# The RWKV recurrence's two exponentials from one clipped difference, and nine small operations of the routing scheduled later

## The chip, the cores and the metric

The kernel runs as one program on one core of a Trainium2 chip. The time is the device time of one execution in microseconds, from its start to the end of its last instruction or transfer. The kernel before was timed nine times: median 370.09 us, lowest 368.94, highest 377.28. The profile beside these times is that of one more execution.

A core has five engines that run at the same time, each through its own list of instructions in order: TensorE (PE: matrix products, with weight loads listed as PEld), VectorE (DVE), ScalarE (ACT), GpSimd (POOL) and SyncE (SP, which here only issues transfers). They wait for each other by semaphores.

## The reference

One layer on 2048 tokens of 512 channels. The normalised input goes into two parts, whose results are added to the input.

```python
xn = _layernorm(x)
# part 1: time mixing; a sequence of 2048 steps in every channel
r, v, k = split(einsum('btc,dc->btd', xn, W_rvk))
def step((p, q, o), (kt, vt)):              # w = -exp(time_decay), u = time_first
    no = maximum(o, u + kt)
    A, Bc = exp(o - no), exp(u + kt - no)
    y = (A * p + Bc * vt) / (A * q + Bc)
    no2 = maximum(w + o, kt)
    A2, B2 = exp(w + o - no2), exp(kt - no2)
    return (A2 * p + B2 * vt, A2 * q + B2, no2), y
attn = einsum('btc,dc->btd', sigmoid(r) * y, W_out)
# part 2: 12 experts, the two likeliest for each token; 8 are real (gate, up, down), 4 return their input
g, u = einsum(xn, gate_w), einsum(xn, up_w)
ffn = sum over the two experts of weight * (down_w of (silu(g) * u)), or weight * xn
out = x + attn + ffn
```

What the change touches is `no2`, `A2` and `B2`: one of the two exponents is always zero, since `no2` is the larger of `w + o` and `kt`.

## The kernel before

**Blocks and units.** The tokens are in four blocks of 512 (b = 0 to 3), the channels in four groups of 128 (c = 0 to 3). The recurrence is worked on in 16 units (b, c), in the order of b, then c: channels on the 128 partitions, 512 steps along the row. `scan(b, c)` is a unit. VectorE copies the state of the group into column 0 of the tile `obv` (L355); a hardware scan gives the maxima `o2` (L359); two operations make the exponents `a2` = w + o - o2 (L361) and `b2` = k - o2 (L362); ScalarE takes the two exponentials in place (L364, L365). Then the scan for the denominators (L371), the product with v (L372), the scan for the numerators (L373), the copies of the last column into the state (L380, L381), three operations that make the quotient's parts (L383 to L385), and the reciprocal in two halves with a product behind the second (L389, L391), which gives `yT`. In all but the last three units the halves are put off and done where `divide_some` is called.

**Products.** Keys, values and receptances of block 0 are made by plain products and by `seven`, those of blocks 1 to 3 by `pair`: seven products instead of eight for a product of 2 x 2 blocks (a scheme like Strassen's), for three matrices side by side. Its order on TensorE is written out in `pair`:

```python
order = "A1 A5 R1 A6 A2 R5 A7 A3 R6 A4 B1 R2 B5 B6 R7 B3 B7 R3 B2 B4 R4".split()
```

Every such product is a pair of passes at L601 (128 x 256), into one of the PSUM banks of `change_banks`: tags gu, p2, p3 and pr have one buffer, p1 has two, and `ps_o` (expert results and the output product) two. Products 2 are added to their destination by VectorE two steps later (`owe`, L633 for one of them); only then is bank p2 free for the next product 2. Most others are copied out by ScalarE (L612 to L645).

**Experts.** 23 tiles of 128 tokens are gathered by GpSimd (L1043, four indirect transfers to a tile, five tiles ahead), turned by VectorE (`turn`, L1101), multiplied by gate and up weights (`up`, L1120, 32 passes of 128 x 128 to a tile), put through the activation (`activate`: ScalarE L1132, VectorE L1133 and L1134), multiplied by the down weights (`finish`, L1085, two passes of 128 x 512), scaled by ScalarE (L1152) and added into the output by GpSimd (L1156). SP fetches the expert's weights, whose number it reads from a table on the chip. Two tiles, the fourth and the eighth, are mixed: their last 32 rows belong to another expert. `mixed_tiles` makes what they need, nine small VectorE operations (L999 to L1019): `late_i`, the addresses of those rows, and `owner_i`, the numbers of the experts, which SP reads in `fetch`.

**Order.** From the normalisation on, the order on every engine is the order in which the program emits instructions (a manual schedule), and in the main stage this comes from a table of due times: `plan(at, work)` lists a generator under a time; the table is sorted, and each entry advances its generator by one step, that is to its next `yield`. The 16 `scan` generators have six steps each: one spacing for the first unit, (-1, 3, 5, 7, 10, 11.5), and for the others (0, 5, 7.5, 9.5, 12, 14) after the unit's start, units being 16.75 apart. `mixed_tiles` is one step, due at 8, in the midst of the first unit; the expert tiles' halves, the products' steps and the output product of blocks 0 to 2 (`attention`, L1253) stand in the same table. The due times are only an order; nothing waits for a clock.

**End.** After the last units of block 3 only the output product of block 3 is left: sixteen groups of four passes at L1253 (the last group in two halves at L1241), each needing `yT` of all four channel groups of its block. Ahead of them on TensorE stand the output products of the rest of block 2.

Of the kernel before, what the change touches and what calls it, by code (L numbers as in the profile page):

```python
# [26 lines left out]
F32 = mybir.dt.float32  # L27
BF16 = mybir.dt.bfloat16
I32 = mybir.dt.int32
AF = mybir.ActivationFunctionType  # L30
ALU = mybir.AluOpType
# [3 lines left out]
P = 128  # L35
# [3 lines left out]
TB = 512  # L39
# [24 lines left out]
def layer(ctx: ExitStack, tc: tile.TileContext, x, w_rvk, w_out, decay, first, cls, ebias, gu, down, out):  # L64
    nc = tc.nc

    def pool(name, bufs, **kw):
        return ctx.enter_context(tc.tile_pool(name=name, bufs=bufs, **kw))
# [141 lines left out]
    for c in range(CC):  # L210

        s = const.tile([P, 5], F32, tag=f"state{c}", name=f"state{c}")
# [131 lines left out]
    def scan(b, c):  # L344

        n = f"{b}_{c}"
        s = state[c]
        w, cf = wdec[:, c : c + 1], cfac[:, c : c + 1]
        k = kvr[b, c, "k"]
        if c == 0:  # L350
            yT[b] = xyp.tile([P, CC, TB], F32, tag="xy", name=f"yT{b}")


        obv = wk1.tile([P, 3, TB + 1], F32, tag="obv", name=f"obv{n}")
        nc.vector.tensor_copy(obv[:, :, 0:1], s[:, 0:3].unsqueeze(2))  # L355
        o, bs, bvs = (obv[:, m, 0:TB] for m in range(3))
        o2, b2, bv = (obv[:, m, 1 : TB + 1] for m in range(3))

        nc.vector.tensor_tensor_scan(o2, w.to_broadcast([P, TB]), k, s[:, 0:1], ALU.add, ALU.max)  # L359
        a2 = wk1.tile([P, TB], F32, tag="a2", name=f"a2{n}")  # L360
        nc.vector.scalar_tensor_tensor(a2, o, w, o2, ALU.add, ALU.subtract)  # L361
        nc.vector.tensor_sub(b2, k, o2)  # L362
        yield
        nc.scalar.activation(a2, a2, AF.Exp)  # L364
        nc.scalar.activation(b2, b2, AF.Exp)  # L365
        yield

        v = kvr[b, c, "v"]
        sums = wk1.tile([P, 2, TB], F32, tag="sums", name=f"sums{n}")
        sq, sp = sums[:, 0, :], sums[:, 1, :]  # L370
        nc.vector.tensor_tensor_scan(sq, bs, a2, s[:, 3:4], ALU.add, ALU.mult)  # L371
        nc.vector.tensor_mul(bv, b2, v)  # L372
        nc.vector.tensor_tensor_scan(sp, bvs, a2, s[:, 4:5], ALU.add, ALU.mult)  # L373

        er = kvr[b, c, "r"]
        if b > 0:
            nc.scalar.activation(er, er, AF.Exp, scale=-1.0)
        num = yT[b][:, c, :]
        if b + 1 < NTB:
            nc.vector.tensor_copy(s[:, 0:3].unsqueeze(2), obv[:, :, TB : TB + 1])  # L380
            nc.vector.tensor_copy(s[:, 3:5].unsqueeze(2), sums[:, :, TB - 1 : TB])  # L381
        yield
        nc.vector.scalar_tensor_tensor(sq, b2, cf, sq, ALU.mult, ALU.add)  # L383
        nc.vector.scalar_tensor_tensor(er, er, 1.0, sq, ALU.add, ALU.mult)
        nc.vector.scalar_tensor_tensor(num, bv, cf, sp, ALU.mult, ALU.add)  # L385
        yield
        def divide(h):
            hs = slice(h * HALF, (h + 1) * HALF)
            nc.vector.reciprocal(er[:, hs], er[:, hs])  # L389
            if h == 1:  # L390
                nc.vector.tensor_mul(num, num, er)  # L391

        for h in range(2):
            divisions.append(lambda h=h: divide(h))
            if (b, c) in units[-3:]:
                divide_some(len(divisions))
                yield
# [4 lines left out]
    def divide_some(n):  # L402
        for _ in range(min(n, len(divisions))):
            divisions.pop(0)()
# [514 lines left out]
    for m, tok in enumerate((tok0, tok1)):  # L919
# [20 lines left out]
        for j in range(NT):  # L940
            k = m * NT + j
# [332 lines left out]
    wk1 = pool("wk1", 1)  # L1274
# [19 lines left out]
    head = False  # L1294
    fill(8)
    stages = [scan(*u) for u in units]
    DONE = 7 + 9 + 16 + 2 + 12
    STEPS = 2 * 2 * CC + 11 * (CC - LEAD) + 21 * (len(units) - CC) // 2
# [8 lines left out]
    def plan(at, what, *args):  # L1307
        table.append((at, iter([(what, *args)]) if callable(what) else what))

    for at in (-1, 3, 5, 7, 10, 11.5):  # L1310
        plan(at, stages[0])
    for u in range(1, len(units)):
        for at in (0, 5, 7.5, 9.5, 12, 14):
            plan((u - 1) * UNIT + 10.5 + at, stages[u])

    middle = attention(NTB - 2)
# [2 lines left out]
            plan((len(units) - 2) * UNIT + 10.5 + at, middle)  # L1319
    plan(3, gather, 3)  # L1320
    plan(3.5, turn, 0)
    plan(8, mixed_tiles)
    plan(4.5, gather, 4)
    one = total / groups / CC
    for m in range(groups):
# [35 lines left out]
    with tc.If(count > TILES):  # L1361
        with tc.For_i(TILES, MAX_TILES, 1) as i:
            cols = {}
            for name, a, dt in (
                ("which", which_i, I32), ("token", token_i, I32), ("to", to_i, I32), ("weight", wplace, F32)
            ):
                if name == "token":
                    shape, at = [P, P // SQ, 1], a[:, :, bass.ds(i, 1)]
                else:
                    shape, at = [P, 1], a[:, bass.ds(i, 1)]  # L1370
# [59 lines left out]
```

## Time and profile before

| what | value |
|---|---|
| median of nine executions | 370.09 us |
| all nine | 377.28, 368.94, 370.74, 369.48, 376.86, 370.63, 369.77, 370.09, 369.48 |
| the profiled execution | 370.26 us, of which the span of the profile is 368.4 |
| PE busy | 358.0 us, 97% of the span |
| VectorE busy | 320.0 us, 87% |
| GpSimd busy | 167.6 us, 45% |
| ScalarE busy | 116.9 us, 32% |
| granted TensorE clock, mean over the span | 0.991 |

By stages, as busy microseconds of each stretch:

| stretch, us | PE | VectorE | ScalarE | GpSimd | clock | DMA share |
|---|---|---|---|---|---|---|
| 0 to 20 (load, normalise) | 18.43 | 14.70 | 9.14 | 7.06 | 1.00 | 0.92 |
| 20 to 60 (first products, routing) | 39.64 | 34.72 | 18.30 | 2.90 | 1.00 | 0.72 |
| 60 to 110 (first units, first expert tiles) | 44.94 | 39.24 | 13.22 | 29.97 | 0.93 | 0.52 |
| 110 to 340 (main stage) | 230.00 | 212.55 | 74.52 | 120.60 | 1.00 | 0.73 |
| 340 to 368 (last units, last output product) | 24.95 | 18.81 | 1.75 | 7.05 | 1.00 | 0.76 |

A row of a group of instructions in the profile reads: line, engine, operation, output and inputs by their names in the program, shapes, count, then busy us and mean ns of one, and the idle time of the engine ahead of them with what ended it. A row of the timeline reads: start in us, length, engine, line, operation, and in brackets how long the engine had waited and for whom. Busy time of PE is modelled from the passes' starts, so a PE at 10.00 of 10 can still pass slowly: the distance between passes shows it.

### The profile page before, as it was taken

Reading aid. Unit: us, or ns where it says so; the run is one execution under the profiler, and the core shown is the slowest. Engines: PE = TensorE matmul, PEld = TensorE weight load, DVE = VectorE, ACT = ScalarE, POOL = GpSimd, SP = SyncE. Lnnn points to the kernel's source line nnn. Section 1 sums busy time; section 2 is a strip of 40 time slices with the busy share of each in tenths; the row PEclk is TensorE's granted clock in tenths of the full one; section 3 lists DMA queues with packets and bytes.
Section 4 is the critical chain, followed back from the end, with each engine's and each line's share of the span. In section 5 each row is a group of like instructions: output and inputs, shape, how many; then the busy total and the mean of one; then the engine's idle time right before and its main releaser. Section 6 shows DMA issues by size and latency. Waiting matters only on the chain. (4 is left out here: it accounts for less than half of the span.)

```text
span 368.4 us, 5356 instructions
## 1 busy us (share of the span) xinstructions
PE 358.0 (97%) x1854; PEld 259.7 (70%) x1854; DVE 320.0 (87%) x555; ACT 116.9 (32%) x263; POOL 167.6 (45%) x192
## 2 busy tenths in 40 slices
PE   8999999999789999999999999999999999999996
PEld 3765577898467679656777788888877788874444
DVE  5879889989389999699999798999999599989981
ACT  3576231333033333323341324432432334231100
POOL 7000300587655756556545186346788522113510
PEclk9999999999969999999999999999999999999999
DMA  7998940439454699666987676697879765933793
GB/s 262 397 390 332 342 142 0 145 86 405 167 190 98 178 337 294 230 165 196 306 286 221 201 213 191 185 246 219 263 229 236 198 163 149 315 55 36 176 187 115
DMA packets 25004, 78.69 MB, mean 214 GB/s; under 512 B 4368, under 2 KB 4752, under 8 KB 21200
## 3 DMA queue, kind: packets, MB, share of 16 engines
q1 hardware_dynamic: 16560, 58.28, 44.9%
q0 software_dynamic: 8416, 20.06, 26.2%
q8 instruction: 15, 0.25, 0.3%
q14 instruction: 13, 0.11, 0.1%
HBM read 63.25 MB, written 19.27 MB: 224 GB/s over the span
## 5 line engine op out<-in xcount | busy, mean ns | idle before, releaser
L1043 POOL DMA_INDIRECT xg<-xs,token_i x92 | 102.8, 1118 | 71.9 <-DVE token_i L984 27.7
L1120 PEld LDWEIGHTS pg<-xgT,gw 128*128 128x128 f32 x672 | 79.6, 194 | 3.4 <-issue 2.2
L1120 PE MATMUL pg<-xgT,gw 128*128 128x128 f32 x672 | 79.8, 277 | 0.0
L1156 POOL DMA_INDIRECT out_dram<-yo,to_i x23 | 39.8, 1732 | 66.4 <-issue 36.6
L1253 PE MATMUL pw<-wout_sb,yT 128*128 128x512 f32 x120 | 54.2, 595 | 0.2 <-PEq L1361 0.2
L389 DVE RECIPROCAL r<-r 128x256 f32<-128x256 f32 x32 | 53.7, 1718 | 0.0
L1085 PE MATMUL po<-dw,act 128*128 128x512 f32 x84 | 40.2, 595 | 0.9 <-issue 0.7
L1253 PEld LDWEIGHTS pw<-wout_sb,yT 128*128 128x128 f32 x120 | 22.2, 190 | 25.7 <-issue 24.5
L1132 ACT ACTIVATE act<-pg 128x256 f32<-128x256 f32 x23 | 8.8, 383 | 80.3 <-PE pg L1120 52.8
L601 PE MATMUL p<-S,wrvk 128*128 128x256 f32 x96 | 25.0, 379 | 1.9 <-issue 1.8
L1152 ACT ACTIVATE yo<-po,wplace 128x512 f32<-128x512 f32 x23 | 15.8, 688 | 34.2 <-PE po L1085 27.2
L1133 DVE SCALAR_TENSOR_TENSOR act<-act,pg 128x256 f32<-128x256 f32 x23 | 9.6, 416 | 19.5 <-ACT act L1132 16.5
L1085 PEld LDWEIGHTS po<-dw,act 128*128 128x128 f32 x84 | 15.9, 190 | 14.6 <-issue 13.7
L601 PE MATMUL p<-xnT,wrvk 128*128 128x256 f32 x96 | 24.8, 381 | 0.8 <-issue 0.8
L601 PE MATMUL p<-S,T 128*128 128x256 f32 x96 | 25.6, 391 | 0.0
L371 DVE TENSOR_TENSOR_SCAN sums<-obv,state,a 128x512 f32<-128x512 f32 x16 | 20.3, 1270 | 3.1 <-ACT obv L365 2.9
L601 PEld LDWEIGHTS p<-S,T 128*128 128x128 f32 x96 | 18.6, 196 | 5.6 <-issue 3.0
L601 PEld LDWEIGHTS p<-xnT,wrvk 128*128 128x128 f32 x96 | 17.8, 190 | 6.4 <-issue 4.2
L601 PEld LDWEIGHTS p<-S,wrvk 128*128 128x128 f32 x96 | 18.0, 190 | 6.1 <-issue 4.0
L373 DVE TENSOR_TENSOR_SCAN sums<-obv,state,a 128x512 f32<-128x512 f32 x16 | 20.5, 1284 | 0.6
L359 DVE TENSOR_TENSOR_SCAN obv<-wdec,state,k 128x512 f32<-128x512 f32 x16 | 20.4, 1276 | 0.0
L1101 DVE STREAM_TRANSPOSE xgT<-xg 128x512 f32<-128x512 f32 x23 | 16.2, 704 | 0.1
(263 smaller groups left out, 565.2 us busy)
## 6 DMA issues: line engine op xcount, KB each, us to landing
gw<-in_gu_dram SPq DMA_DIRECT2D x25, 1024.0 KB
dw<-in_down_dram SPq DMA_DIRECT2D x25, 512.0 KB
x<-in_x_dram SPq DMA_DIRECT2D x16, 256.0 KB
xs<-x SPq DMA_DIRECT2D x16, 256.0 KB
wrvk<-in_w_rvk_dram SPq DMA_DIRECT2D x3, 1024.0 KB
xrow<-xs SPq DMA_DIRECT2D x8, 256.0 KB
out_dram<-xrow POOLq DMA_DIRECT2D x8, 256.0 KB
xrows<-xs SPq DMA_DIRECT2D x8, 256.0 KB
```

Source lines behind the costliest of these rows:

```text
L359: nc.vector.tensor_tensor_scan(o2, w.to_broadcast([P, TB]), k, s[:, 0:1], ALU.add, ALU.max)
L371: nc.vector.tensor_tensor_scan(sq, bs, a2, s[:, 3:4], ALU.add, ALU.mult)
L373: nc.vector.tensor_tensor_scan(sp, bvs, a2, s[:, 4:5], ALU.add, ALU.mult)
L389: nc.vector.reciprocal(er[:, hs], er[:, hs])
L601: nc.tensor.matmul(dst, rows_(k), a[:, k, :], start=(first and k == 0), stop=(k == 1), skip_group_check=True,)
L1043: nc.gpsimd.indirect_dma_start(out=xg[:, h, :], out_offset=None, in_=quarters, in_offset=bass.IndirectOffsetOnAxis(ap=token[:, h, column(i ...
L1085: nc.tensor.matmul(out_, lhs[:, c, :], rhs[0][:, c, :], start=(c == 0), stop=(c == last))
L1101: nc.vector.transpose(xgT.rearrange("p c (h i) -> p h c i", i=SQ), st[i]["xg"].rearrange("p h (c j) -> p h c j", j=SQ),)
L1120: nc.tensor.matmul(pg[:, c // IC, c % IC * P : (c % IC + 1) * P], w[0][:, k, rs], xgT[:, k, :], start=(k == 0), stop=(k == CC - 1),)
L1152: nc.scalar.activation(yo, po, AF.Identity, scale=weight[:, column(i) : column(i) + 1])
L1156: nc.gpsimd.indirect_dma_start(out=out, out_offset=bass.IndirectOffsetOnAxis(ap=index, axis=0), in_=yo[ps], in_offset=None, compute_op=ALU ...
L1253: nc.tensor.matmul(po, yT[b][:, c, j * P : (j + 1) * P], wout_sb[:, c, :], start=(c == 0), stop=(c == CC - 1),)
```

## The change

The exponents are no longer made apart. One operation makes the difference d = w + o - k; ScalarE makes B2 as exp(-relu(d)) and A2 as exp(-relu(-d)), in two pairs of passes, each in a step of its own, so that `scan` has seven steps for six and the tables of due times have one entry more. The subtraction at L362 goes. The two sums are written into the tile of the maxima and weights, which has five rows for three, so that the head copy takes all five columns of the state (before three) and the two copies back become one. The product with v comes ahead of the first sum's scan, and the quotient's first part goes into `a2`. `mixed_tiles` is due at 12.5 for 8, which in the order of VectorE puts its nine operations behind the first scan of the second unit, and behind the last steps of the first unit.

```diff
--- before.py
+++ after.py
@@ -351,25 +351,27 @@
             yT[b] = xyp.tile([P, CC, TB], F32, tag="xy", name=f"yT{b}")
 
 
-        obv = wk1.tile([P, 3, TB + 1], F32, tag="obv", name=f"obv{n}")
-        nc.vector.tensor_copy(obv[:, :, 0:1], s[:, 0:3].unsqueeze(2))
+
+        obv = wk1.tile([P, 5, TB + 1], F32, tag="obv", name=f"obv{n}")
+        nc.vector.tensor_copy(obv[:, :, 0:1], s.unsqueeze(2))
         o, bs, bvs = (obv[:, m, 0:TB] for m in range(3))
-        o2, b2, bv = (obv[:, m, 1 : TB + 1] for m in range(3))
+        o2, b2, bv, sq, sp = (obv[:, m, 1 : TB + 1] for m in range(5))
 
         nc.vector.tensor_tensor_scan(o2, w.to_broadcast([P, TB]), k, s[:, 0:1], ALU.add, ALU.max)
         a2 = wk1.tile([P, TB], F32, tag="a2", name=f"a2{n}")
-        nc.vector.scalar_tensor_tensor(a2, o, w, o2, ALU.add, ALU.subtract)
-        nc.vector.tensor_sub(b2, k, o2)
-        yield
-        nc.scalar.activation(a2, a2, AF.Exp)
-        nc.scalar.activation(b2, b2, AF.Exp)
+        nc.vector.scalar_tensor_tensor(a2, o, w, k, ALU.add, ALU.subtract)
+        yield
+
+        nc.scalar.activation(b2, a2, AF.Relu)
+        nc.scalar.activation(b2, b2, AF.Exp, scale=-1.0)
+        yield
+        nc.scalar.activation(a2, a2, AF.Relu, scale=-1.0)
+        nc.scalar.activation(a2, a2, AF.Exp, scale=-1.0)
         yield
 
         v = kvr[b, c, "v"]
-        sums = wk1.tile([P, 2, TB], F32, tag="sums", name=f"sums{n}")
-        sq, sp = sums[:, 0, :], sums[:, 1, :]
+        nc.vector.tensor_mul(bv, b2, v)
         nc.vector.tensor_tensor_scan(sq, bs, a2, s[:, 3:4], ALU.add, ALU.mult)
-        nc.vector.tensor_mul(bv, b2, v)
         nc.vector.tensor_tensor_scan(sp, bvs, a2, s[:, 4:5], ALU.add, ALU.mult)
 
         er = kvr[b, c, "r"]
@@ -377,13 +379,13 @@
             nc.scalar.activation(er, er, AF.Exp, scale=-1.0)
         num = yT[b][:, c, :]
         if b + 1 < NTB:
-            nc.vector.tensor_copy(s[:, 0:3].unsqueeze(2), obv[:, :, TB : TB + 1])
-            nc.vector.tensor_copy(s[:, 3:5].unsqueeze(2), sums[:, :, TB - 1 : TB])
-        yield
-        nc.vector.scalar_tensor_tensor(sq, b2, cf, sq, ALU.mult, ALU.add)
-        nc.vector.scalar_tensor_tensor(er, er, 1.0, sq, ALU.add, ALU.mult)
+            nc.vector.tensor_copy(s.unsqueeze(2), obv[:, :, TB : TB + 1])
+        yield
+        nc.vector.scalar_tensor_tensor(a2, b2, cf, sq, ALU.mult, ALU.add)
+        nc.vector.scalar_tensor_tensor(er, er, 1.0, a2, ALU.add, ALU.mult)
         nc.vector.scalar_tensor_tensor(num, bv, cf, sp, ALU.mult, ALU.add)
         yield
+
         def divide(h):
             hs = slice(h * HALF, (h + 1) * HALF)
             nc.vector.reciprocal(er[:, hs], er[:, hs])
@@ -1307,10 +1309,10 @@
     def plan(at, what, *args):
         table.append((at, iter([(what, *args)]) if callable(what) else what))
 
-    for at in (-1, 3, 5, 7, 10, 11.5):
+    for at in (-1, 2.5, 3.5, 5, 7, 10, 11.5):
         plan(at, stages[0])
     for u in range(1, len(units)):
-        for at in (0, 5, 7.5, 9.5, 12, 14):
+        for at in (0, 4.5, 6, 7.5, 9.5, 12, 14):
             plan((u - 1) * UNIT + 10.5 + at, stages[u])
 
     middle = attention(NTB - 2)
@@ -1319,7 +1321,7 @@
             plan((len(units) - 2) * UNIT + 10.5 + at, middle)
     plan(3, gather, 3)
     plan(3.5, turn, 0)
-    plan(8, mixed_tiles)
+    plan(12.5, mixed_tiles)
     plan(4.5, gather, 4)
     one = total / groups / CC
     for m in range(groups):
```

## The prediction, made before the changed kernel was run

> **What bounds the kernel now.** I read the busy times stage by stage first (columns: stretch; PE, weight loads, VectorE, ScalarE, GpSimd busy us with counts; granted TensorE clock; DMA share; GB/s), then the chain that ended last.
>
> ```profile
> 90.00:100.00 10.00, 8.32 (x42) 5.73 (x41) 5.04 (x5) 1.19 (x2) 7.73 (x8) 1.00 0.63 229
> 100.00:110.00 10.00, 7.46 (x30) 6.10 (x29) 7.08 (x13) 2.79 (x8) 4.53 (x5) 0.66 0.55 173
> ...
> 140.00:150.00 10.00, 10.00 (x59) 8.42 (x58) 9.90 (x17) 2.63 (x7) 4.38 (x3) 1.00 0.84 271
> ```
> ```profile
> 345.10 16.55 PE pw L1253 x38
> 361.65 1.73 PE pw L1241 x8
> ```
>
> PE is busy 10.00 of 10 us in every stretch from 110 to 340, and the chain ends on PE alone. VectorE is close behind (9.90 in 140 to 150), ScalarE has room (2.63). So VectorE time saved between 110 and 340 buys nothing by itself: the PE order, and those of SP and GpSimd, are the same in both programs, instruction for instruction. Time can only come from the holes in PE, and be lost by new holes. The holes are two. The first:
>
> ```profile
> 85.73 0.15 DVE L999 TENSOR_SCALAR late<-tok_p 128x1 f32<-128x1 f32 x1
> ...
> 87.32 0.17 DVE L1019 CAST owner_i<-owner 128x4 int32<-128x4 f32 x1
> 87.40 0.41 DVE L633 TENSOR_TENSOR r<-r,p2r 128x256 f32<-128x256 f32 x1
> ...
> 87.87 1.13 PE L601 MATMUL p<-xnT,wrvk 128*128 128x256 f32 x4 [0.84 <-issue]
> ```
>
> The product at 87.87 needs the bank that L633 empties (it has one buffer), and L633 stands behind the nine small operations on the mixed tiles. A product before it began at 86.00, and four passes take 0.86 (85.14 to 86.00), so it could have begun at 86.87: 1.00 us lost. The second hole is larger:
>
> ```profile
> 95.30 1.38 PE L1085 MATMUL po<-dw,act 128*128 128x512 f32 x2
> 97.40 1.27 PE L1085 MATMUL po<-dw,act 128*128 128x512 f32 x2 [0.72 <-issue]
> ...
> 103.37 1.22 PE L601 MATMUL pr<-xnT,wrvk 128*128 128x256 f32 x2 [1.41 <-ACT r L641]
> ```
>
> Eight passes fill the 8.07 us from 95.30 to 103.37; undisturbed (114.12 to 116.70) the same eight take 2.58. ScalarE waits 11.2 us before its activation at 102.40, for a product that PE finished at about 92.5: PE's signals arrive ten us late and together. The clock then stands at half: the next eight passes take 3.58 us (103.37 to 106.95) for 1.73, and the 32 of the second expert tile 4.58 (106.95 to 111.53) for 3.58 (88.83 to 92.41). Together 5.5 + 1.85 + 1.0 = 8.35 us. No row says what holds the signals; they come back 0.8 us after the last gather of that series has landed (101.6).
>
> **The change part by part.** Rows for it:
>
> ```profile
> L362 DVE TENSOR_TENSOR obv<-k,obv 128x512 f32<-128x512 f32 x16 | 11.0, 685 | 0.0
> L380 DVE COPY state<-obv 128x3 f32<-128x3 f32 x12 | 1.7, 144 | 0.0
> L365 ACT ACTIVATE obv<-obv 128x512 f32<-128x512 f32 x16 | 10.0, 627 | 0.0
> L255 ACT ACTIVATE x<-x,shift,rstd 128x512 f32<-128x512 f32 x8 | 6.2, 809 | 6.5 <-DVE shift L248 6.5
> ```
>
> *VectorE.* Each of 16 units loses the subtraction (0.685), and 12 lose one of two state copies (0.144): 11.0 + 1.7 = 12.7 us off 320. It lies in the stage where PE sets the pace, so 0 on the path. Nothing else changes its length: the scans write into one tile of five rows, the wider head copy has 5 columns for 3.
>
> *ScalarE.* Two exponentials become four passes. Relu is in no row. Lower bound 0.627 (L365, same shape and memory), upper 0.809 (L255, which takes two columns of numbers besides); I take 0.63, since Relu here takes none. A table switch would add 1.283 each time (the row of the load at L759); the built program still has two loads, so 0. Sum 32 x 0.63 = 20 us on an engine busy 117 of 368: hidden in the middle, by this count: the copies out of PE's banks end 1.1 us or more before PE writes there again in all but one unit of the middle stage, mostly 2.9, and where four passes now stand in a row, PE is on expert tiles whose results go to VectorE much later. The exception (0.57 before 135.47) keeps its place ahead of the new passes. If that cover were gone, a unit would cost 1.3.
>
> *The chain inside a unit.* Before, the second scan waits for both exponentials: 327.23 to 328.38 in the last unit but one. Now: Relu 0.63, Exp 0.63 behind it (it reads its result; 0.05 for the wait, as 0.04 to 0.09 between engines in the rows), then the second pair one pitch (0.53) after the first Exp: 0.68 + 0.53 + 0.68 + 0.63 = 2.52 for 1.15, so 1.37 later; the product with v (0.67) now runs during that wait. Net 0.70 per unit wherever VectorE arrives early. In the middle it finds room: the transposed tokens of an expert tile are ready 2.3 us or more before PE wants them, except 1.41 at 151.4 and 0.24 at 172.5, and ahead of both VectorE has been relieved of two subtractions (in the first case against one wait of 1.4, leaving 0.8).
>
> *The tail* has no such room, as nothing but these units is left:
>
> ```profile
> 340.52 0.63 ACT L364 ACTIVATE a<-a 128x512 f32<-128x512 f32 x1 [6.86 <-DVE a L361]
> ...
> 341.79 1.28 DVE L371 TENSOR_TENSOR_SCAN sums<-obv,state,a 128x512 f32<-128x512 f32 x1
> ...
> 352.58 0.68 DVE L391 TENSOR_TENSOR yT<-yT,r 128x512 f32<-128x512 f32 x1
> ```
>
> The last two units follow each other on VectorE with no idle time from 328.4 on, and at 326.5 VectorE waits for PE, so it can't start sooner. The last y is there at 353.27. PE's last 14 passes of block 2 and 6 of block 3 come before the one that needs it: 345.10 + 20 x 0.43 = 353.7. Room 0.45. Two units by 0.70 make y 1.4 later (in the last unit 0.61 to 0.70), so PE stops 0.9 us: lower bound 0.5 (1.0 less the room, if half of the wait is absorbed), upper 1.9 with Relu at 0.81 (0.36 more per unit, and PE needs it at the same place).
>
> *The moved operations.* They issue nine VectorE operations (1.74 us, 85.73 to 87.49) and no DMA. Behind the second unit's first scan, L633 follows L385 at once and ends at 86.2; PE's first hole of 1.00 closes. The numbers of the mixed tiles come at about 86.2 + 0.16 + 1.28 + 0.75 + 1.74 = 90.1, 2.6 later. SP waits for them with one weight load (issued 88.14, then 90.8); behind it on SP is a load that waits for PE until 102.63, and the weights are used at 118.52. GpSimd reads the late addresses much later still. Cost 0; without that cover 2.6.
>
> **Sum.** Closed hole -1.00; tail +0.9; ScalarE and VectorE in the middle 0. The open question is whether the 1.00 survives. PE would come to the second hole 1.00 earlier. If that hole ends with the gathers, which GpSimd issues every 1.25 us whatever PE does, PE still goes on at 103.37, and the 1.00 is only more waiting. I take this, because of the 0.8 us between the last landing and the release. The profiled execution took 370.26 (span 368.4, 1.9 around it), the median is 370.09; so 370.09 + 0.9 = **371.0**, with 370.6 to 372.0 as this case's own range.
>
> [...]
>
> **Rivals.** (1) *The gain is kept*: the second hole begins and ends with PE's own work, so all shifts by 1.00. For it: the hole begins while PE runs without a pause. Against: the release after the last landing. 370.09 - 1.00 + 0.9 = 370.0. (2) *The second hole goes*: a shift of 1.0 us on PE and 2.6 on one weight load moves it apart from whatever holds the signals. For it: no other stretch from 110 on shows one. Against: seven of nine times lie within 0.5%, so it comes every time. 370.09 - 8.35 - 1.00 + 0.9 = 361.6. (3) *ScalarE is dearer*: the place is the chain of the last two units, the price 0.36 for Relu at 0.81 and 0.4 for two waits of 0.2 on its own results, per unit; from 0.45 late on PE pays all. 371.0 + 2 x 0.76 = 372.5. (4) *The change doesn't relieve anything*: that is half of the forecast already, as PE sets the pace.
>
> **How the numbers follow.** Forecast 0.40, (1) 0.30, (2) 0.14, (3) 0.16. What a measurement here can tell from no change is some 0.2%, 0.74 us: 369.35 to 370.83. Faster: (2) and a third of (1): 0.24. Same: the rest of (1) and a fifth of the forecast: 0.28. Slower: the rest, 0.48. The range takes in (2) at the low end and most of (3) at the high one, 361.4 to 372.4, with a little of (3) and of unlooked-for stalls left out.
>
> **What would show it.** In the changed profile: the product after 86.0 starts at 86.9 with no idle time; PE goes on at about 103.4 (forecast), 102.4 (rival 1) or keeps its pace through 95 to 103 (rival 2); Relu rows of 0.63; a PE hole of about 0.9 us in the attention of block 3 that ends with VectorE's last yT (rival 3: 2.4); PE at 10.00 of 10 between. A hole of PE in the middle, ended by a ScalarE copy, would make the count of room wrong.

## The result, and the profile after

The changed kernel takes 374.26 us (median of 20 executions, 369.92 to 381.44); the kernel before, measured beside it, 370.20 us (62 executions). The ratio is 1.0097, 95% interval 1.0079 to 1.0114: slower by 1.0%, outside the predicted range. Here about one execution in ten of either kernel takes 2 to 9 us longer, in later sets up to 9 of 17 of the kernel before; the ratios leave these out, the medians do not.

The profiled execution took 374.91 us, its span is 373.1 where it was 368.4. By stages (columns as before: stretch; PE, weight loads, VectorE, ScalarE, GpSimd busy with counts; granted clock; DMA share; GB/s):

```profile
80.00:90.00 10.00, 6.23 (x33) 4.66 (x31) 8.04 (x17) 1.50 (x4) 7.87 (x8) 1.00 0.98 379
90.00:100.00 10.00, 5.75 (x36) 5.10 (x37) 4.70 (x9) 2.74 (x6) 7.22 (x8) 0.97 0.59 193
100.00:110.00 10.00, 9.11 (x28) 7.00 (x28) 8.29 (x14) 3.25 (x8) 4.48 (x5) 0.69 0.15 36
```

From 110 to 340 PE stands at 10.00 of 10 as before. What is new lies from 80 to 100: PE was busy 9.16 and 8.32 there, now 6.23 and 5.75. The stretch of before that the prediction does not show, and the timeline of that place before, on ScalarE, which copies what PE has finished:

```profile
80.00:90.00 10.00, 9.16 (x56) 8.09 (x55) 8.82 (x23) 2.66 (x8) 7.70 (x8) 1.00 0.91 343
```
```profile
81.89 0.38 ACT L1132 ACTIVATE act<-pg 128x256 f32<-128x256 f32 x1 [3.62 <-PE pg L1120]
...
87.07 0.37 ACT L645 COPY morer<-pr 128x256 f32<-128x256 f32 x1 [0.49 <-issue]
...
102.40 0.38 ACT L1132 ACTIVATE act<-pg 128x256 f32<-128x256 f32 x1 [11.20 <-PE p L601]
```

The same place now:

```profile
81.11 1.03 PE L603 MATMUL p<-S,wrvk 128*128 128x256 f32 x4
...
83.06 0.39 ACT L1134 ACTIVATE act<-pg 128x256 f32<-128x256 f32 x1 [4.03 <-PE p L603]
...
85.87 0.37 ACT L631 COPY more<-p 128x256 f32<-128x256 f32 x1 [2.43 <-remote]
...
86.30 1.13 PE L603 MATMUL p<-S,wrvk 128*128 128x256 f32 x4 [2.43 <-ACT more L631]
...
93.04 0.37 ACT L647 COPY more<-p 128x256 f32<-128x256 f32 x1 [3.19 <-remote]
...
94.41 0.27 PE L1122 MATMUL pg<-xgT,gw 128*128 128x128 f32 x1 [0.40 <-issue]
95.13 0.27 PE L1122 MATMUL pg<-xgT,gw 128*128 128x128 f32 x1 [0.46 <-issue]
...
102.12 0.39 ACT L1134 ACTIVATE act<-pg 128x256 f32<-128x256 f32 x1 [1.40 <-PE pg L1122]
```

This is the second hole of the prediction, but it opens earlier. The passes of the first expert tile end at 81.3, and ScalarE sees that only at 83.06, 1.8 us late; in the kernel before the signals (PE's raising of the semaphore on which ScalarE waits) were on time up to 87. From 83 on PE waits for copies that wait for PE's own late signals, and from 94 on its passes of 0.11 us come 0.7 us apart, then in groups of two to four with pauses of up to 1.9 us. It is over at 102.1, where it was over before (102.4), with less work done meanwhile: the first mixed tile's product, at 118.52 before, is at 121.45, 2.93 later. The tail:

```profile
347.89 8.82 PE L1255 MATMUL pw<-wout_sb,yT 128*128 128x512 f32 x20
...
355.68 0.65 DVE L1221 SCALAR_TENSOR_TENSOR orows<-xrows,zw,orows 128x512 f32<-128x512 f32 x1
...
356.25 0.68 DVE L393 TENSOR_TENSOR yT<-yT,r 128x512 f32<-128x512 f32 x1
...
356.99 7.99 PE L1255 MATMUL pw<-wout_sb,yT 128*128 128x512 f32 x18 [0.27 <-DVE yT L393]
```

The pass at 347.89 is the first behind a branch in PE's list, where every profile has a pause of 0.31 us; it serves as a mark. At the branch PE is 2.79 later than before (347.89 for 345.10); the last yT then costs it 0.54 (VectorE's last addition at 368.47, 3.33 after the 365.14 of before). The remaining 1.37 of the 4.7 lies behind it: from that addition to the end of the span it is now 4.6 us, before 3.3. Here the output's last block is read back at 351.27, 8 us later than before, since GpSimd's last scatter starts at 346.08 and not at 337.82, and the first three writes of its rows are issued within 2.90 us and not 5.54. That the late writes make up the 1.37 is likely; no run tests it. So: hole 2.79, tail 0.54, last transfers 1.37.

The costs of the edits are as expected. The four passes on ScalarE (busy us, mean ns):

```profile
L365 ACT ACTIVATE obv<-a 128x512 f32<-128x512 f32 x16 | 10.1, 631 | 12.4 <-DVE a L362 12.4
L366 ACT ACTIVATE obv<-obv 128x512 f32<-128x512 f32 x16 | 10.1, 631 | 0.5
...
L369 ACT ACTIVATE a<-a 128x512 f32<-128x512 f32 x16 | 10.1, 630 | 0.5
L368 ACT ACTIVATE a<-a 128x512 f32<-128x512 f32 x16 | 9.9, 620 | 0.0
```

Relu (L365, L368) takes 620 to 631 ns, as an exponential does (630 and 631); ScalarE goes from 116.9 to 135.8 us, VectorE from 320.0 to 309.8.

### The profile page after: what moved, and what is told of

It is laid out like the page before. It is cut to its first block, busy times and chain, and to the rows that moved or that the text cites. A ratio compares the mean times of both kernels' runs of the same rounds, so it can differ in the third digit from the quotient of the medians.

```text
span 373.1 us, 5334 instructions
## 1 busy us (share of the span) xinstructions
PE 356.7 (96%) x1854; PEld 259.4 (70%) x1854; DVE 309.8 (83%) x527; ACT 135.8 (36%) x295; POOL 163.5 (44%) x192
## 5 line engine op out<-in xcount | busy, mean ns | idle before, releaser
L1045 POOL DMA_INDIRECT xg<-xs,token_i x92 | 99.3, 1079 | 79.1 <-DVE token_i L986 27.7
L374 DVE TENSOR_TENSOR_SCAN obv<-obv,state,a 128x512 f32<-128x512 f32 x16 | 20.5, 1280 | 6.7 <-ACT a L369 5.9
L1087 PEld LDWEIGHTS po<-dw,act 128*128 128x128 f32 x84 | 16.0, 190 | 12.8 <-issue 11.5
L375 DVE TENSOR_TENSOR_SCAN obv<-obv,state,a 128x512 f32<-128x512 f32 x16 | 20.2, 1263 | 0.0
L373 DVE TENSOR_TENSOR obv<-obv,v 128x512 f32<-128x512 f32 x16 | 10.9, 679 | 8.0 <-ACT obv L366 7.3
```

The lines of the kernel that those rows point to most:

```text
L1045: nc.gpsimd.indirect_dma_start(out=xg[:, h, :], out_offset=None, in_=quarters, in_offset=bass.IndirectOffsetOnAxis(ap=token[:, h, column(i ...
L1087: nc.tensor.matmul(out_, lhs[:, c, :], rhs[0][:, c, :], start=(c == 0), stop=(c == last))
```

## The experiments

Seven sets of runs, each on one chip with its own runs of the kernel before. The chips gave a surprise that governs all the rest: in four sets the kernel before took 361.4 to 361.8 us and had no second hole, in three 370.2 to 375.5.

| kernel | us | before, same set | ratio, 95% interval |
|---|---|---|---|
| changed kernel (the result) | 374.26 | 370.20 | 1.0097, 1.0079 to 1.0114 |
| changed kernel again (after_again) | 378.94 | 375.48 | 1.0112, 1.0034 to 1.0189 |
| last two units in the old form (a_tail) | 377.09 | 375.48 | 1.0125, 1.0072 to 1.0177 |
| the same again (a_tail2) | 378.86 | 372.24 | 1.0157, 1.0094 to 1.0220 |
| move, and VectorE's tail in another order (best2) | 371.12 | 372.24 | 0.9998, 0.9963 to 1.0032 |
| move alone (b_move) | 361.21 | 361.66 | 0.9978, 0.9965 to 0.9992 |
| move alone (b_move2) | 361.88 | 361.80 | 1.0005, 0.9968 to 1.0042 |
| clipped recurrence alone (a_unmove) | 362.20 | 361.66 | 1.0014, 1.0003 to 1.0025 |
| clipped recurrence alone (a_unmove2) | 361.94 | 361.80 | 1.0015, 1.0001 to 1.0029 |
| clipped recurrence alone (a_unmove3) | 361.85 | 361.71 | 0.9998, 0.9969 to 1.0026 |
| changed kernel (after2) | 361.53 | 361.80 | 1.0022, 0.9984 to 1.0060 |
| three gather buffers (b_gathers) | 361.88 | 361.66 | 1.0001, 0.9985 to 1.0016 |
| first run of gathers cut (b_break) | 361.75 | 361.80 | 1.0012, 0.9979 to 1.0046 |
| first run of gathers cut (b_break3) | 363.82 | 361.71 | 1.0024, 0.9997 to 1.0051 |
| later weights (b_weights) | 361.59 | 361.66 | 0.9997, 0.9986 to 1.0008 |
| later weights (b_weights2) | 361.63 | 361.40 | 1.0001, 0.9978 to 1.0023 |
| two gather buffers, kernel before (b_two) | 364.98 | 361.40 | 1.0060, 1.0021 to 1.0099 |
| two gather buffers, changed kernel (a_two) | 365.63 | 361.40 | 1.0031, 0.9987 to 1.0076 |
| two gather buffers, move, tail (best) | 371.99 | 361.40 | 1.0125, 1.0089 to 1.0161 |

The first five rows are the sets with the hole. The expectations below call it a matter of the chip. That is too much: the set of b_move (361.66) and that of best2 (372.24) ran on the same chip.

**The parts, one at a time.** The move alone is one line on the kernel before, its undoing the reverse on the changed one.

```diff
-    plan(8, mixed_tiles)
+    plan(12.5, mixed_tiles)
```

> The kernel before with the nine operations on the mixed tiles moved alone (due at 12.5). Theory A (the clipped recurrence brings the loss; the late signals of PE began at 81.3 us, ahead of the place where the nine operations stood): the first hole of 1.00 us at 86.9 closes, PE goes on after the stall at 102 to 104 as before, time 369 to 370.5, ratio to the kernel before 0.996 to 1.001. Theory B (the move brings it): the stall begins by 82 to 85 and PE is 3 us later from 120 on, time 373 to 374, ratio 1.008 to 1.011.

> The changed kernel with the nine operations back at their old place (due at 8): the clipped recurrence alone. Theory A: slower than before by 1.0% or a little more, 373.5 to 375, PE's signals late from some 81 us on. Theory B: 370.6 to 371.5, that is the tail of 0.5 to 0.9 us alone, with signals late from 90 us on only.

There was no hole in this set, so it couldn't tell theory A from B; it gives the price of each part without the hole. The move gains 0.2% here (its second run, below, shows no gain), the clipped recurrence loses 0.14%. Where the move's 1.00 us goes is seen in its second run (b_move2):

> The move of the nine operations alone, again, for a chip on which the kernel before takes 370 us or more. There, theory A (the clipped recurrence makes the hole longer): ratio 0.996 to 1.002. Theory B (the move does): ratio 1.007 to 1.012. Without the hole both say 0.997 to 0.999, as in the first run of this kernel.

```profile
136.09 0.75 DVE L385 SCALAR_TENSOR_TENSOR yT<-obv,cfac,sums 128x512 f32<-128x512 f32 x1
...
136.76 0.41 DVE L633 TENSOR_TENSOR k<-k,p 128x256 f32<-128x256 f32 x1
...
137.22 1.13 PE L601 MATMUL p<-xnT,wrvk 128*128 128x256 f32 x4 [0.26 <-DVE k L633]
```

The product at 87 starts without a wait, but 50 us later another product finds the same bank p2 full: L633 stands behind a unit's L385, and the distance between passes is 0.42 too long there (0.43 in b_move, at 137.01). A PE that runs 1.0 us earlier meets VectorE's next deadline. Net 0.57 to 0.58 on PE; the median of this run doesn't show it (361.88 for 361.80), that of b_move does.

> The clipped recurrence alone, again, for a chip with the hole. There, theory A: ratio 1.007 to 1.013; theory B: 1.000 to 1.003. Without the hole both say 1.001 to 1.002, as in the first run.

> The clipped recurrence alone, once more, for a chip with the hole. There, theory A: ratio 1.007 to 1.013; theory B: 1.000 to 1.003. Without the hole both say 1.001 to 1.002.

None of the three met the hole. All show the old first hole (1.07 to 1.15) and the same wait in the tail. In the first (a_unmove):

```profile
344.68 0.65 DVE L1221 SCALAR_TENSOR_TENSOR orows<-xrows,zw,orows 128x512 f32<-128x512 f32 x1
345.25 0.68 DVE L393 TENSOR_TENSOR yT<-yT,r 128x512 f32<-128x512 f32 x1
...
345.99 4.56 PE L1255 MATMUL pw<-wout_sb,yT 128*128 128x512 f32 x10 [0.29 <-DVE yT L393]
```

The passes stand 0.45 further apart there (0.63 and 0.45 in the other two); from 110 to 340 PE has no new hole. That is what 32 more passes on ScalarE cost without the hole: the tail, nothing in the middle.

**The whole change, again.**

> The changed kernel unaltered, beside the kernel before on one chip. The four runs so far fell on a chip where the kernel before takes 361.7 us and shows no second hole (PE busy 10.00 of 10 from 90 to 110). Theory C (the change itself is worth about nothing, and the loss of 1% is a second hole that the change makes longer on the chip that has it): where the kernel before takes 361 to 362, the changed one takes 361.0 to 361.6, ratio 0.998 to 1.000 (move alone -0.8, clipped recurrence alone +0.5); where the kernel before takes about 370, the changed one takes 373.5 to 375. Theory D (the clipped recurrence costs by itself, wherever it runs): 364 to 366 on a chip without the hole, ratio 1.008 to 1.011.

> The changed kernel unaltered. Theory C (worth about nothing by itself, and the 1% is a longer hole): on a chip where the kernel before takes 361 to 362, ratio 0.998 to 1.000 (the move -0.8 us, the clipped recurrence +0.5); on one where it takes 370 or more, ratio 1.008 to 1.013. Theory D (the clipped recurrence costs by itself everywhere): 1.008 or more on both.

The first met the hole: 1.1% slower. The second did not: 361.53 for 361.80, no difference that can be told. Its profile shows what the prediction hoped for and nothing in its way:

```profile
80.00:90.00 10.00, 10.00 (x66) 9.28 (x65) 9.65 (x23) 4.40 (x10) 7.61 (x8) 1.00 0.94 356
90.00:100.00 10.00, 10.00 (x59) 8.42 (x58) 9.90 (x14) 3.93 (x9) 7.63 (x8) 1.00 0.89 296
100.00:110.00 10.00, 10.00 (x61) 7.25 (x63) 9.63 (x13) 1.66 (x4) 8.11 (x7) 1.00 0.53 153
```
```profile
85.69 0.41 DVE L635 TENSOR_TENSOR r<-r,p2r 128x256 f32<-128x256 f32 x1
...
86.77 1.03 PE L603 MATMUL p<-xnT,wrvk 128*128 128x256 f32 x4
...
88.07 0.15 DVE L1001 TENSOR_SCALAR late<-tok_p 128x1 f32<-128x1 f32 x1
```

The first hole is closed, and PE is busy 10.00 of 10 through the whole place with the same transfers (356 and 296 GB/s, 343 and 229 before). A wait of 0.41 at 119.64 and 0.46 in the tail give most of it back. Theory C fits both runs; D, which asked for 1.008 or more without the hole, falls (1.0022, at most 1.0060).

**The last two units in the old form**, two exponentials and an own subtraction there, the rest as changed:

```diff
+        old = (b, c) in units[-2:]
-        nc.vector.scalar_tensor_tensor(a2, o, w, k, ALU.add, ALU.subtract)
+        nc.vector.scalar_tensor_tensor(a2, o, w, o2 if old else k, ALU.add, ALU.subtract)
+        if old:
+            nc.vector.tensor_sub(b2, k, o2)
...
+        if old:
+            nc.scalar.activation(a2, a2, AF.Exp)
...
+        if old:
+            nc.scalar.activation(b2, b2, AF.Exp)
```

> The changed kernel with the last two of the 16 units in the old form (two exponentials, own subtraction). Theory E (what the clipped recurrence costs is the chain of four passes in the last two units, where PE waits 0.45 us for the last yT): that wait goes, and the time falls by 0.4 to 0.6 us under the changed kernel on the same chip. Theory F (it costs in the middle of the stage, or in the ScalarE copies): the time stays that of the changed kernel.

> The changed kernel with the last two units in the old form, again, for a chip without the hole. Theory E (the clipped recurrence costs the wait of 0.45 us ahead of the last yT and nothing else): no such wait in the profile, PE without a pause of its own from 110 us to the end but for 0.31 at the branch, median 360.7 to 361.2 where the kernel before takes 361.7, ratio 0.997 to 0.999. Theory F (the cost lies elsewhere): the wait goes and the time stays at that of the changed kernel, ratio 0.9995 or more.

Both met the hole, which is several us long and varies, so the times don't tell E from F. The profiles do in part: the wait ahead of the last yT is gone in both, as E says; that the time without the hole falls with it is not shown. The times tell something else: with 14 of 16 units clipped the loss is there (1.6% in a_tail2), so the hole's growth doesn't come from the last two units. The 1.3% of a_tail says less: the medians of all executions in its set, 377.09 and 375.48, lie 0.4% apart. The hole itself, in a_tail:

```profile
78.94 0.37 ACT L634 COPY k<-p 128x256 f32<-128x256 f32 x1 [0.60 <-remote]
...
86.12 0.59 PE L615 MATMUL pr<-S,R 128*128 128x256 f32 x2 [0.40 <-issue]
...
92.86 0.94 POOL L1057 DMA_INDIRECT xg<-xs,token_i  x1 [0.30 <-issue]
...
96.12 0.38 ACT L1146 ACTIVATE act<-pg 128x256 f32<-128x256 f32 x1 [15.62 <-remote]
...
96.82 2.08 PE L615 MATMUL p<-S,wrvk 128*128 128x256 f32 x4 [10.11 <-ACT more L643]
```

In the record PE's semaphore is raised at 78.91, then not for 17 us, then four times from 96.10 to 96.28; ScalarE waits 15.6 us, PE 10.1. The last gather of the run landed at 95.38.

**What holds the signals.** Three edits were meant for this: fewer buffers for gathered tokens, so that GpSimd's first unbroken run of gathers is shorter; the third expert's weights later, so that the burst of transfers is; and the run cut after twelve gathers.

```diff
-    gathered = pool("gathered", 4)
+    gathered = pool("gathered", 3)
```
```diff
-        while fetched[what] < min(ahead[i] + 3, len(parts)):
+        while fetched[what] < min(ahead[i] + 3 - (i == 0), len(parts)):
```
```diff
+        if i == 1:
+            mark = const.tile([P, 1], F32, tag="mark", name="mark")
+            nc.gpsimd.tensor_copy(mark[0:1, :], st[2]["xgT"][0:1, 0, 0:1])
+            for m in (3, 4, 5):
+                gather(m)
-        if i + 5 < n:
+        if 0 < i and i + 5 < n:
             gather(i + 5)
...
-    plan(3, gather, 3)
-    plan(4.5, gather, 4)
```

> The kernel before with three buffers for the gathered tokens in place of four: the first unbroken run of gathers is 20 long, not 24, and ends some 5 us earlier, since the sixth tile's gathers wait for the third tile's transpose. Theory G (the second hole lasts as long as GpSimd's run of gathers): PE's signals come back at about 97, not 102.4, and the time falls by 4 to 6 us, to 364 to 366. Theory W (the hole comes from the burst of expert weights that fills the DMA engines from 80 to 95): nothing changes there, 369.5 to 371.

> The kernel before with the third expert's weights fetched one tile later at the start (1.5 MB less in the burst that fills the DMA engines from 80 to 95 us). Theory W: the second hole shrinks or goes, 362 to 367. Theory G: signals come back with the last gather at about 102 as before, 369.5 to 371.

> The kernel before with the third expert's weights fetched one tile later at the start, as before, now for a chip with the hole. Theory W, on such a chip: 362 to 367; theory G: the signals come back with the last gather as in the kernel before, within 1 us of it.

> The kernel before with its four buffers kept, but the gathers of the fourth to sixth tile held until the third tile's transpose (a one-element copy on GpSimd that reads it): the first run of gathers is 12 long and ends near 89, not 24 and near 100. Theory G, on a chip with the hole: PE's signals come back 0.7 to 1.3 us after the twelfth gather has landed, by 92, and the time falls by 5 to 9 us, to 361 to 366. Theory W: 369 or more. Without the hole: 361 to 362.5 by both, the gathers of the fourth tile coming just in time.

> The kernel before with the first run of gathers cut to 12, once more, for a chip with the hole. Theory G there: PE's signals come back 0.7 to 1.3 us after the twelfth gather has landed, and the time falls by 5 us or more under the kernel before on the same chip. Theory W: within 1.5 us of it. Without the hole: within 0.3% of it by both, as in the first run.

All five fell in sets without the hole, so theories G and W were not tested. They show only that the edits cost nothing that can be told there, and that weights, gathers and PE's passes in this density do not make the hole by themselves.

**Two buffers, and a version to beat both.** Gathers three tiles ahead into two buffers, on both kernels; then with the move and with VectorE's tail reordered by a factor that depends on yT:

```diff
-    gathered = pool("gathered", 4)
+    gathered = pool("gathered", 2)
...
-        if i + 5 < n:
-            gather(i + 5)
+        if i + 3 < n:
+            gather(i + 3)
...
-    plan(3, gather, 3)
-    plan(4.5, gather, 4)
```
```diff
+        late_zw = const.tile([P, NJ], F32, tag="late_zw", name="late_zw")
+        nc.vector.scalar_tensor_tensor(
+            late_zw, yT[b][:, CC - 1, TB - NJ :], 0.0, zw[:, b * NJ : (b + 1) * NJ], ALU.mult, ALU.add
+        )
...
-                orows[i], xrows[i], zw[:, i : i + 1], orows[i], ALU.mult, ALU.add
+                orows[i], xrows[i], late_zw[:, j : j + 1], orows[i], ALU.mult, ALU.add
```

> The changed kernel with two buffers for the gathered tokens and gathers three tiles ahead (before: four and five), so that GpSimd's first unbroken run of gathers is 12 to 16 long, and each later tile's four wait for a transpose. Theory G (on a chip with the second hole, PE's signals are held until a run of gathers has landed; in the last profile they came 0.7 us after the last landing, 95.4 and 96.1): on such a chip the hole ends by 88 to 92 or does not open, and the time falls by 5 us or more under the changed kernel's 374 to 379, to about that of the kernel before or under it. Theory W (the hole comes from the weights alone): within 1 us of the changed kernel. On a chip without the hole: 361 to 362 by both.

> The same two edits on the kernel before. Theory G, on a chip where the kernel before takes 370 or more: 362 to 366; theory W: 370 or more. On a chip without the hole: 361 to 362.5 by both.

> The kernel before with the nine operations moved, gathers in two buffers, and VectorE's additions of the output's last block held behind the last yT (they stood ahead of it and wait for a transfer; in two profiles PE waited 3.7 and 4.6 us for that). Without the hole 360.5 to 361.3 (the 1.00 us of the first hole, less some waits), and no execution near 368; with the hole, theory G: 362 to 365.

> The kernel before with the nine operations moved, and VectorE's additions of the input to the output's last block held behind the last yT (a four-element operation that reads yT makes their factor); the gathers as before. If the late executions near 368 come from that addition standing ahead of the last yT and waiting for a transfer: none of them near 368, median 360.6 to 361.2, ratio 0.997 to 0.999. If they have another cause: one in ten near 368 as in the kernel before.

Two buffers are a loss in b_two and best; a_two's interval takes in 1. Best, in a set without the hole, took 365.17 to 378.47 where 360.5 to 361.3 was expected. In its profile (an execution of 378.47 us):

```profile
237.24 3.63 POOL L1229 DMA_DIRECT2D out_dram<-xrow  x4 [8.59 <-DMA out_dram<-yo,to_i]
...
252.35 1.62 POOL L1156 DMA_INDIRECT out_dram<-yo,to_i  x1 [6.31 <-DMA out_dram<-xrow]
252.61 0.71 DVE L1101 STREAM_TRANSPOSE xgT<-xg 128x512 f32<-128x512 f32 x1 [12.87 <-DMA xg<-xs,token_i]
...
253.43 2.90 PE L1120 MATMUL pg<-xgT,gw 128*128 128x128 f32 x12 [13.97 <-issue]
```

GpSimd's accumulation of block 0 into the output falls between the gathers, the gathers behind it land late, and with three tiles of lead in place of five VectorE and PE wait 13 and 14 us. In a_two the same wait of VectorE is 6.93 us (at 240.1); in the profile of b_two (362.26 us) and in those with five tiles of lead there is none of over 2 us between 105 and 340. The last version (best2) keeps four buffers and five tiles. It met the hole: 0.9998 of the kernel before, so it does not beat it by anything that can be told. Its purpose was the executions near 368. What makes one of them long is seen in b_move's profile (368.84 us, the only one of its runs over 361.6):

```profile
345.44 1.77 SPq L1218 DMA_DIRECT2D orows<-out_dram  x4
...
348.15 0.75 DVE L1219 SCALAR_TENSOR_TENSOR orows<-xrows,zw,orows 128x512 f32<-128x512 f32 x1 [5.12 <-DMA orows<-out_dram]
348.82 0.68 DVE L391 TENSOR_TENSOR yT<-yT,r 128x512 f32<-128x512 f32 x1
...
349.56 10.68 PE L1253 MATMUL pw<-wout_sb,yT 128*128 128x512 f32 x18 [4.58 <-DVE yT L391]
```

GpSimd's last scatter starts at 340.12 here, in b_move2 at 328.0; so the read of the output is late, VectorE waits 5.12 us for it with the last yT queued behind, and PE waits 4.58. Its next passes then come 0.85 us apart for 0.43, with the clock at half (348.18 to 355.01), and VectorE's last addition is at 363.73, in b_move2 at 356.43: 7.3 later. In best2 that order is gone; one execution of 13 still took 378.33, and in its profile PE has no such wait, but a long hole. Whether the executions near 368 are gone without the hole was not seen. Of both kernels and all versions, the move alone is the only one with an interval under 1 (b_move), and its repetition doesn't confirm it.

## Why the prediction was wrong

**The direction** was the likeliest one, the size was not: 374.26 for 371.0, and over the range's end of 372.4. Of the sum's terms the tail was too large; the second hole and the last transfers, both put at 0, cost 2.79 and 1.37.

**VectorE and ScalarE.** Predicted 12.7 us off VectorE. Its rows sum to 12.5 less (345.4 before, 332.9 after); its busy time, in which rows that overlap count once, falls by 10.2. Predicted 20 us more on ScalarE with Relu at 0.63; the rows sum to 19.8 more, busy time rises by 18.9, with Relu at 0.62 to 0.63. The upper bound of 0.81 and rival 3 fall; its wait of 0.2 on ScalarE's own results is in no row: in the last unit the exponential starts 0.66 after the Relu of 0.63 that it reads (343.99, 344.65).

**The first hole** closes as predicted wherever the second is absent: the product starts at 86.77, 86.9 was named. The sum had the whole 1.00; 0.41 to 0.43 of it comes back as a new wait further on. The search for room in the middle looked for results that become late, and not for PE that becomes early.

**The tail** was over-sized: predicted yT 1.4 later and PE stopped for 0.9; measured 0.88 later (356.93 against 353.26 and PE's 2.79) and 0.44 on the pass that waits, 0.54 in all, 0.45 to 0.63 in the sets without the hole. The chain from the first exponent to the second scan is 1.18 longer (343.96 to 346.50, before 340.43 to 341.79), not 1.37: before, the end of the subtraction L362 stood in it too.

**The second hole** is where the forecast failed. It priced the hole by its end: it "ends with the gathers", so PE goes on at the same moment and an earlier PE only waits longer. For the move this fits: with the hole, best2 (the move and the other tail order) is at 0.9998. The step that failed is "ScalarE and VectorE in the middle 0". It took the hole's beginning for given, as if nothing but the moved operations touched it. In the changed kernel the signals are late from 81 on and not only after 87, the hole ends where it did, and less work fits in front of it: 2.79 us at the branch, where the sum had 0.

In the four further profiles with the hole it opens early too. In after_again (382.83 us), a_tail (375.17) and a_tail2 (381.02), all with clipped units, the last signal before the stop is raised at 78.5 to 78.9 (in a_tail2 the next was due at 82.5); in best2 (378.33), without clipped units, at 79.3:

```profile
79.33 0.37 ACT L620 COPY k<-p 128x256 f32<-128x256 f32 x1 [0.71 <-remote]
...
96.50 0.38 ACT L1132 ACTIVATE act<-pg 128x256 f32<-128x256 f32 x1 [16.80 <-remote]
```

At the branch, against 336.40 without the hole (b_weights), PE is late by 8.7 us in before, 11.5 in after, 13.6 in a_tail, 15.0 in after_again, 16.4 in best2 and 18.0 in a_tail2. So a hole that opens early goes with a late PE. The profile of best2, the longest of its 13 executions, shows that it can do so without clipped units; with them every profile has it so. (Of after_again's time, a wait in the tail like that of b_move, 3.68 us here, is another part.) Which part of the change does it, a_tail2 and best2 tell in one set: both have the move, the one with 14 clipped units loses 1.6%, the one with none loses nothing. That speaks for theory A. It is not shown for the clipped recurrence without the move, which never met the hole.

**Rival 2**, that the hole vanishes and 361.6 is left, was right about the size: without the hole the kernel before takes 361.4 to 361.8. It was wrong about the cause: the kernel before loses it as well, in other sets. The argument against it, that the hole comes every time in nine executions, was no argument on its cause: nine that all have it can't show what it hangs on.

**What stays open:** why the hole is there in one set and not in another, what holds PE's signals, and by what the clipped units open it earlier, if it is they alone. That it ends with the gathers is a coincidence in time that five profiles show and none tests:

| profile with the hole | last landing of the run of gathers | PE's signals back |
|---|---|---|
| before | 101.59 | 102.37 |
| after | 100.75 | 102.10 |
| after_again | 95.03 | 96.14 |
| a_tail | 95.38 | 96.10 |
| best2 | 95.13 | 96.48 |

In after (from 83.04 on) and in a_tail2 (90.88, 100.87) single signals come in between; in a_tail2 the rest come from 103.03 on. And in after_again, a_tail and best2 GpSimd's run stops after twenty gathers, not 24, because it waits for a transpose that waits for PE, so the order of cause may be the other one.

## What to carry to other kernels

A hole whose cause no row of the profile shows has two ends, and both are unknown: give its growth a price of its own, even for edits that only shift what lies around it. Before explaining a hole, see whether the unchanged kernel has it in another set of runs; here it was worth 8.7 us (the branch at 345.10 before, at 336.40 in b_weights) and came and went. And where an engine sets the pace, a hole that is closed is worth what remains after the next deadline of the engine just behind it, here 0.57 of 1.00.

## What the runs showed of the hardware

The hole comes with missing records. In the six profiles that have it, PE's semaphore shows 230 to 237 updates (232 in before, 237 in after), though 253 instructions raise it, and VectorE's 405 to 449 for 452 to 470; in the profiles without it there are at least as many as instructions. The passes themselves are all recorded (1854 in every profile). In best2 passes of 128x128 and of 128x256 alike begin 0.71 or 0.72 us apart in it (below). What loses the records, and whether it also holds the signals, is not shown: every execution has a recorded span and clock, so none without recording stands beside them.

The stretches at half clock (granted 0.50; in before from 102.23 to 109.06, in after from 99.31 to 106.14) have lengths in one step. Apart from the last of each profile, which the end cuts off, they are 6.83 us long in before, after and b_move, 10.24 in a_tail, 13.65 and 3.41 in after_again, 3.41 in a_two, and 17.07 in a_tail2, best2 and best: one to five times 3.41. In a_tail PE's last passes before the stop begin at 86.12, the clock falls at 89.78 and comes back at 100.02, 3.2 us after PE goes on. In best2 it fell without such a stop of PE:

```profile
82.19 0.36 PE L1120 MATMUL pg<-xgT,gw 128*128 128x128 f32 x1 [0.45 <-issue]
82.91 0.27 PE L1120 MATMUL pg<-xgT,gw 128*128 128x128 f32 x1 [0.35 <-issue]
83.62 0.47 PE L601 MATMUL p<-S,wrvk 128*128 128x256 f32 x1 [0.44 <-issue]
84.33 0.38 PE L601 MATMUL p<-S,wrvk 128*128 128x256 f32 x1 [0.24 <-issue]
85.05 0.70 PE L601 MATMUL p<-S,wrvk 128*128 128x256 f32 x2 [0.34 <-issue]
```

The clock fell at 85.96; in the 3.41 us before, one such step, PE had begun five passes, at most 0.72 us apart. What makes the clock fall is not shown by these two.
